# First image loaded and normalised first, VectorE's order fixed until the first attention, relative logits and convolution in turn in pieces twice as long

## The chip, the cores and the metric

The kernel runs on one core of a Trainium2 chip. The metric is the device time in microseconds (us) of one execution, the median of several. The core has five engines that run side by side, each with its own queue of instructions that it takes in order: TensorE (PE; its weight loads are listed apart as PEld), VectorE (DVE), ScalarE (ACT), GpSimd (POOL) and SyncE (SP, which here only issues DMA transfers). TensorE writes its results to PSUM, from where VectorE or ScalarE copies them to SBUF.

## What is computed

The input x holds 8 images of 32 x 32 pixels with 256 channels, in float32. Each image goes through two layers. Layer 0 is a group norm, then a 3 x 3 convolution to 192 channels beside a self-attention over the 1024 pixels, with 8 heads of 8 channels, whose logits have relative terms in both directions. Layer 1 is a self-attention over 1024 tokens with 128 channels, and a mixture of 8 experts of which 2 are used per image.

```python
x = x + conv_attn(group_norm(x))
t = to_tokens(x)
t = t + attn(ln(t))
t = t + moe(ln(t))
```

The parts of `conv_attn` that matter here:

```python
conv_out = conv3x3(x, conv_w) + conv_b
k, q, v = split(x @ qkv_w + qkv_b); q = q * 8 ** -0.5
logits = q @ k.T + rel_w(q, key_rel_w) + rel_h(q, key_rel_h)
attn = softmax(logits) @ v
return concat([conv_out, attn @ attn_w + attn_b])
```

## The kernel before

The kernel has a first phase, with both attentions, image by image, and a second phase with the experts for all images. The first phase is software-pipelined over images by hand: the order of TensorE's instructions is exactly the order in which the program is written (`tc.manual_schedule` at L876 with PE alone), while a scheduler with a cost model orders the other engines' instructions when the kernel is built.

Before the loop over images, the program sets up constants and prepares image 0. In the order of the code:

- `load_image(0)` (L112) loads image 0 into the tile T by a DMA that GpSimd issues (L105).
- ACT issues the loads of `qkvw` and of the convolution weights `taps` (1.7 MB, L125). VectorE (L130 to L133) and ScalarE (L134, L135) turn these nine taps into `convw`: sums and differences for a convolution that makes pairs of neighbouring pixels from shared products.
- SP issues the small loads: `kqb`, `vb`, the biases `l0b`, `aw`, layer 1's `wqkv1`, `wo`, `bo`, and at the end (L181) the two relative tables, 2 KB each.
- VectorE makes small selection matrices from the identity (`gsel`, `gavg`, `esel`, `hsel`), and from the relative tables the weights `bdh` and `bdw` (L194). `reld` (L205, L208) holds differences of rows of `bdh`; VectorE and GpSimd make it together. `KM` (L228, L229, GpSimd) holds for each head group a pattern of ones to which 16 small DMAs add the keys (L358).
- `norm_steps(0)`: TensorE transposes image 0 (`tpx`, L270), VectorE copies it out (L271), takes statistics (L275, L277), TensorE averages over groups (`pm`, `pv`), and VectorE writes the normalised image into `gpad` (L299), which has a border for the convolution. GpSimd adds the biases to T (L279).
- `by_tiles` makes the copy x of `gpad` (GpSimd, L320) that `v` needs, `by_pairs` the sums and differences `gdif` for the convolution (L311).
- `input_steps(0)`: keys and queries (`pk`, L334, into `kq`), values (`pvv`, L367), then the relative logits `prel` (L406): 256 small matmuls of 32 rows and 64 columns in four quarters, (width, height) x (half 0, half 1). After each quarter VectorE and ScalarE copy one half each out (L418, L420). The width part `rw` goes to DRAM (`rwd`) and is transposed by TensorE (`tpw`, L431) into `rwq`. Last, it creates the first `Unit`, whose tile F is gathered by 40 DMAs.

Then for each image b, `conv_layer_attention` runs the attention of layer 0 in four units of 512 queries and two head groups each, with the convolution of the image as filler at its two ends. While it ends, `ahead()` normalises image b+1. `attention_layer` then runs layer 1's attention, and its gaps are filled by `fill(us)`: it takes steps from `input_steps(b + 1)` until their listed times add up to `us`. A step of `prel` is listed with 0.7 us and is followed by `conv.run(3)`, three matmuls of image b+1's convolution. So, once per image b = 0 to 6, relative logits and convolution of image b+1 run in turn. A stretch has 16 such turns: a turn has 16 `prel` matmuls and 3 `pc` matmuls of the program. Every float32 matmul stands as two records in the trace, so that a turn shows 32 and 6. In eight of the turns, two transposes `tpn` of layer 1's normalised tokens (L700) stand between. The PSUM tile `pc` holds twelve convolution matmuls; outside `conv_layer_attention` it comes from a pool with one buffer (`po`), so that VectorE must have added it to T (L461 or L463 and twice L467) before the next one starts.

The calls that set where the turns fall are these:

```python
fill(7.5)          # L689, before the tokens are transposed
fill(0.7)          # L702, after each of the 8 token tiles
fill(5.6)          # L706, before queries and keys of layer 1
fill(0.8)          # L812, in the loop over layer 1's scores
```

Pools that matter: `st` has three PSUM buffers, `lg` (which `prel` uses) two, `F` three in SBUF; `taps`, x, `rw`, F, `qkv` and `pr` all take turns in the latter.

Of the kernel before, what the change touches and what calls it, by code (L numbers as in the profile page):

```python
# [9 lines left out]
FP = mybir.dt.float32  # L10
I32 = mybir.dt.int32
AF = mybir.ActivationFunctionType
ALU = mybir.AluOpType
# [3 lines left out]
P = 128  # L17
# [3 lines left out]
KC = C // P  # L21
NH, DH, DK = 8, 8, 64
HG = 4
NG = NH // HG
CO = C - DK
U = 128
E, F = 8, 512
# [8 lines left out]
def kernel(  # L36
# [26 lines left out]
    nc = tc.nc  # L63
    xt = x.rearrange("b h w c -> b (h w) c")
# [26 lines left out]
    with ExitStack() as ph:  # L91
# [11 lines left out]
        def load_image(b):  # L103
            t = work.tile([P, NT, C], FP, tag="T", name="T", bufs=2)
            nc.gpsimd.dma_start(out=t.rearrange("p (r j) c -> p r j c", j=2), in_=xt[b].rearrange("(r p j) c -> p r j c", p=P, j=2))  # L105
            return t
# [9 lines left out]
        def st_tile(name):  # L116
            return ps_st.tile([P, 512], FP, tag="st", name=name)


        qkvw = wp.tile([P, KC, 3 * DK], FP, tag="qkvw", name="qkvw")  # L120
        nc.scalar.dma_start(out=qkvw, in_=qkv_w.rearrange("(k p) o -> p k o", p=P))


        taps = work.tile([P, 4096], FP, tag="F", name="taps", bufs=3)[:, 0 : 9 * KC * CO]
        nc.scalar.dma_start(  # L125
            out=taps.rearrange("p (n o) -> p n o", o=CO), in_=conv_w.rearrange("a b (k p) o -> p (a b k) o", p=P)
        )
        taps = taps.rearrange("p (a b n) -> p b a n", a=3, b=3)
        convw = wp.tile([P, 4, 3, KC * CO], FP, tag="convw", name="convw")
        nc.vector.tensor_tensor(convw[:, 2], taps[:, 0], taps[:, 2], ALU.add)  # L130
        nc.vector.tensor_tensor(convw[:, 0], convw[:, 2], taps[:, 1], ALU.add)
        nc.vector.tensor_tensor(convw[:, 1], convw[:, 2], taps[:, 1], ALU.subtract)
        nc.vector.tensor_scalar(convw[:, 0:2], convw[:, 0:2], 0.5, None, ALU.mult)  # L133
        nc.scalar.copy(convw[:, 2], taps[:, 0])  # L134
        nc.scalar.mul(convw[:, 3], taps[:, 2], -1.0)  # L135
        convw = convw.rearrange("p v a (k o) -> p v a k o", o=CO)

# [10 lines left out]
        nc.sync.dma_start(out=l0b[:, 0, 0:CO], in_=conv_b.partition_broadcast(P))  # L148
        nc.sync.dma_start(out=l0b[:, 0, CO:C], in_=attn_b.partition_broadcast(P))
        aw = wp.tile([DK, DK], FP, tag="aw", name="aw")  # L150
        nc.sync.dma_start(out=aw, in_=attn_w)
# [5 lines left out]
        bo = wp.tile([P, 1, C], FP, tag="bo", name="bo")  # L157
        nc.sync.dma_start(out=bo[:, 0, :], in_=b_o.partition_broadcast(P))


# [14 lines left out]


        rel = []
        for n, table in (("h", key_rel_h), ("w", key_rel_w)):
            M = table.shape[0]
            raw = wp.tile([M, DH], FP, tag=f"raw{n}", name=f"raw{n}")  # L180
            nc.sync.dma_start(out=raw, in_=table)  # L181
            rep = work.tile([P, 2048], FP, tag="pt", name=f"rep{n}", bufs=4)[0:M, 0:P].rearrange(
                "m (r d) -> m r d", d=DH
            )
            nc.vector.tensor_copy(rep, raw.unsqueeze(1).to_broadcast([M, P // DH, DH]))
            pt = st_tile(f"relt{n}")
            nc.tensor.transpose(pt[:, 0:M], rep.rearrange("m r d -> m (r d)"), ident[0:M, 0:M])
            if n == "h":
                bd = work.tile([P, 2048], FP, tag="pt", name="bdh", bufs=4)[:, 0 : M * HG]
                bd = bd.rearrange("p (m h) -> p m h", h=HG)  # L190
            else:
                bd = wp.tile([P, M, HG], FP, tag="bdw", name="bdw")
            for h in range(HG):
                nc.vector.tensor_scalar(bd[:, :, h], pt[:, 0:M], hsel[:, h : h + 1], None, ALU.mult)  # L194
            rel.append(bd)
        bdh, bdw = rel
        bdw = bdw.rearrange("p m h -> p (m h)")

        def half_w(rows, m, k):
            return bdw[rows, (m + 16 * k) * HG : (m + 16 * k + 16) * HG]  # L200


        NM = 48
        reld = wp.tile([P, NM, 16, HG], FP, tag="reld", name="reld")
        nc.gpsimd.tensor_copy(reld[:, :, 0, :], bdh[:, 0:NM, :])  # L205
        for j in range(1, 16):
            eng = nc.vector if j % 2 else nc.gpsimd
            eng.tensor_tensor(reld[:, :, j, :], bdh[:, j : j + NM, :], bdh[:, 0:NM, :], ALU.subtract)  # L208
        reld = reld.rearrange("p m j h -> p m (j h)")

        def half_h(rows, m, k):
            return reld[rows, m + 16 * k, :]

        KM = []
        oh = wp.tile([P, 16 + DH], FP, tag="oh", name="oh")
        nc.vector.tensor_copy(oh[:, 0:1], esel[:, 0:1])  # L220
        nc.vector.tensor_tensor(oh[:, 1:16], esel[:, 1:16], esel[:, 0:1].to_broadcast([P, 15]), ALU.add)
        nc.vector.tensor_copy(oh[:, 16:24], esel[:, 24:32])
        for i in range(NG):
            km = wp.tile([P, 2, 4, P], FP, tag=f"km{i}", name=f"km{i}")
            for a in range(2):
                kv = km[:, a].rearrange("p g (y x) -> p g y x", y=8)
                for g in range(4):
                    nc.gpsimd.tensor_copy(kv[:, g], oh[:, 0:16].unsqueeze(1).to_broadcast([P, 8, 16]))  # L228
                    nc.gpsimd.tensor_tensor(  # L229
                        kv[:, g], kv[:, g], oh[:, 16:24].unsqueeze(2).to_broadcast([P, 8, 16]), ALU.add  # L230
                    )
            KM.append(km)

# [24 lines left out]
        def f_tile(name):  # L258
            return work.tile([P, 2, 4, 512], FP, tag="F", name=name, bufs=3)


# [64 lines left out]
        def input_steps(b, held):  # L326
# [66 lines left out]
            for which in range(2):  # L393
                for half in range(2):
                    prs = lg_tile("prel")
                    for i in range(16):
                        a = half * 16 + i
                        for g in range(NG):
# [6 lines left out]
                            for k in range(2):  # L405
                                nc.tensor.matmul(  # L406
                                    dst[64 * k : 64 * k + 64], lhsT=table(rows, m, k), rhs=mov, start=True, stop=True
                                )
                        if i % 4 == 3 and i < 15:
                            yield 0.7, True  # L410
                    for g in range(NG):
# [9 lines left out]
                    if which == 0 and half == 1:  # L421
                        for g in range(NG):
                            nc.sync.dma_start(out=rwd[g], in_=rw[g])
                    yield 0.7, True

# [449 lines left out]

        with tc.manual_schedule(engines={mybir.EngineType.PE}):  # L876
            held = {}
            for _ in norm_steps(0):
                pass
            held.update(by_tiles())  # L880
            by_pairs()
            for _ in input_steps(0, held):
                pass
            conv = Conv(0)
            means = []
            for b in range(B):
# [26 lines left out]
                def fill(us):  # L913

                    while us > 0:
                        took, small = next(steps, (None, None))
                        if took is None:
                            break
                        us -= took
                        if small:  # L920
                            conv.run(3)

# [287 lines left out]
```

## Time and profile before

| | |
|---|---|
| median of 3 runs | 2516.28 us (2516.07 to 2519.02) |
| profiled execution, its own time | 2525.62 us |
| its span in the trace | 2523.4 us |
| TensorE busy | 2388.8 us, 95% of the span |
| VectorE busy | 1450.5 us, 57% |
| ScalarE busy | 980.1 us, 39% |
| GpSimd busy | 449.8 us, 18% |
| mean granted TensorE clock | 0.982 |

The profile is of one execution, recorded by the chip. The span runs from the first to the last recorded instruction; the execution's own time is 2.2 us longer, and it lies 9.3 us above the median of the timed runs. Times in the timelines are counted from the span's start. Each line of a timeline merges neighbouring instructions of a kind: start, duration, engine, line of the code, operation, output and input tiles with shapes, count, and in brackets how long the engine was idle before it and what released it. The granted clock is the share of full TensorE clock that the chip let through. Matmuls are pipelined, so a matmul's duration is longer than the distance between two starts.

### The profile page before, as it was taken

The page shows a single profiled execution, that of the slowest core. Times are in us where ns is not written, and L with a number is a line of the kernel's source. Part 1 is how long each engine was busy: PE and PEld are TensorE (multiplying, and loading weights), DVE is VectorE, ACT ScalarE, POOL GpSimd, SP SyncE. Part 2 cuts the span into 40 slices and gives each one's busy share as a digit, 9 for nine tenths or more (in the row PEclk, how much of TensorE's full clock was granted, in tenths as well). Part 3 has the DMA queues.
Part 4 walks back from the last instruction along what each step waited for, and adds up shares of the span by engine and source line. Part 5 has one row for each costly group of instructions (what it writes and reads, how often), then busy time and mean ns, then how long its engine had stood idle before and what let it go on. Part 6 is the DMA issues. An engine that isn't in the chain of part 4 may idle for free. (4 is left out here: it accounts for less than half of the span.)

```text
span 2523.4 us, 42411 instructions
## 1 busy us (share of the span) xinstructions
PE 2388.8 (95%) x17657; PEld 1369.0 (54%) x17657; DVE 1450.5 (57%) x2507; ACT 980.1 (39%) x1625; POOL 449.8 (18%) x464
## 2 busy tenths in 40 slices
PE   3999999999999999999999999999999869999998
PEld 2734753475357535643664366436642546666665
DVE  5675377547744874487358735873684434444444
ACT  1065225532553254336333623363346322332222
POOL 6002120302040204010310121012200132222221
PEclk9899999999999999999999989999999879999999
DMA  2440243024202420341044104410430031221110
GB/s 82 91 65 4 50 90 51 7 51 98 40 22 42 96 38 22 61 84 28 23 80 79 15 22 80 78 15 22 84 65 8 1 122 67 75 76 67 67 59 25
DMA packets 73518, 135.86 MB, mean 54 GB/s; under 512 B 12000, under 2 KB 24168, under 8 KB 71280
## 3 DMA queue, kind: packets, MB, share of 16 engines
q1 hardware_dynamic: 67408, 114.42, 21.7%
q0 software_dynamic: 3328, 16.78, 2.0%
q8 instruction: 139, 2.28, 0.4%
q10 hardware_dynamic: 2592, 1.97, 0.3%
q14 instruction: 51, 0.42, 0.1%
HBM read 53.43 MB, written 25.17 MB: 31 GB/s over the span
## 5 line engine op out<-in xcount | busy, mean ns | idle before, releaser
L560 ACT ACTIVATE PT<-st 128x512 f32<-128x512 f32 (+1 forms) x944 | 541.5, 633 | 581.7 <-PE st L552 579.0
L520 DVE TENSOR_REDUCE my<-lg 128x32 f32<-128x1024 f32 x512 | 617.8, 1223 | 159.9 <-PE st L552 126.8
L552 PE MATMUL st<-F,km 32*128 32x512 f32 x2048 | 549.9, 640 | 14.6 <-DMA F<-mb 8.7
L512 PE MATMUL lg<-km,F 24*128 24x512 f32 x2048 | 526.5, 636 | 1.1 <-issue 0.8
L452 PE MATMUL pc<-convw,gdif 128*128 128x192 f32 x1536 | 308.4, 344 | 10.6 <-DVE T L467 10.6
L569 PE MATMUL po<-PT,vall 128*32 128x256 f32 (+1 forms) x3200 | 314.4, 452 | 2.4 <-ACT PT L560 2.4
L452 PEld LDWEIGHTS pc<-convw,gdif 128*128 128x128 f32 x1536 | 250.5, 193 | 79.0 <-issue 72.7
L512 PEld LDWEIGHTS lg<-km,F 24*128 24x128 f32 x2048 | 151.4, 183 | 175.9 <-issue 101.4
L569 PEld LDWEIGHTS po<-PT,vall 128*32 128x32 f32 x3200 | 67.0, 108 | 313.7 <-issue 280.3
L552 PEld LDWEIGHTS st<-F,km 32*128 32x128 f32 x2048 | 179.6, 183 | 92.4 <-issue 42.4
L1123 PE MATMUL phd<-n2T,w 128*128 128x512 f32 x512 | 223.7, 595 | 0.0
L1140 PE MATMUL py<-w,hT 128*128 128x256 f32 x1024 | 223.6, 379 | 0.0
L1140 PEld LDWEIGHTS py<-w,hT 128*128 128x128 f32 x1024 | 194.6, 190 | 33.2 <-issue 7.7
L279 POOL TENSOR_TENSOR T<-T,l0b 128x2048 f32<-128x2048 f32 x8 | 36.2, 4520 | 813.8 <-PE tpx L270 813.8
L1123 PEld LDWEIGHTS phd<-n2T,w 128*128 128x128 f32 x512 | 97.1, 191 | 114.8 <-issue 107.7
L1147 DVE TENSOR_TENSOR r<-py,n 128x256 f32<-128x256 f32 x64 | 27.1, 424 | 214.7 <-PE py L1140 214.6
L784 PE MATMUL po<-pt,qkv 128*128 128x256 f32 x512 | 116.6, 381 | 11.3 <-DVE pt L776 11.3
L1130 ACT ACTIVATE hT<-phd,b1c 128x512 f32<-128x512 f32 x128 | 86.3, 686 | 96.5 <-PE phd L1123 96.3
L762 DVE TENSOR_REDUCE nm<-lg 128x1 f32<-128x1024 f32 x64 | 78.0, 1219 | 72.5 <-PE lg L753 72.5
L753 PE MATMUL lg<-qkv 128*128 128x512 f32 x256 | 119.1, 593 | 0.0
L784 PEld LDWEIGHTS po<-pt,qkv 128*128 128x128 f32 x512 | 96.6, 190 | 36.2 <-DVE pt L776 13.2
L701 POOL TENSOR_TENSOR T<-T,n 128x256 f32<-128x256 f32 x64 | 47.1, 742 | 293.7 <-DVE n L696 293.7
(231 smaller groups left out, 2467.2 us busy)
## 6 DMA issues: line engine op xcount, KB each, us to landing
F<-rh SPq DMA_DIRECT2D x256, 128.0 KB
F<-kq SPq DMA_DIRECT2D x256, 64.0 KB
F<-rwd SPq DMA_DIRECT2D x256, 64.0 KB
w<-in_L_ffn_W_dram SPq DMA_DIRECT2D x32, 512.0 KB
T<-in_x_dram POOLq DMA_DIRECT2D x8, 1024.0 KB, 5.9
rwd<-rw SPq DMA_DIRECT2D x16, 512.0 KB
Td<-T POOLq DMA_DIRECT2D x8, 1024.0 KB, 8.0
T<-Td SPq DMA_DIRECT2D x8, 1024.0 KB
```

The costliest lines, as they stand in the source:

```text
L452: nc.tensor.matmul(pc[:, v, :], lhsT=gflat[:, 2 * pair + v, kc, at : at + P], rhs=convw[:, 2 * pair + v, dy, kc, :], start=i == 0, stop=i ...
L512: nc.tensor.matmul(lg[:, a, :], lhsT=self.F[r : r + 24, a, 0, i * P : (i + 1) * P], rhs=KM[self.g][r : r + 24, a].rearrange("p e k -> p (e ...
L520: nc.vector.tensor_reduce(my[:, :, hl], lg.rearrange("p a (y x) -> p y a x", y=WW), AX.XY, ALU.max)
L552: nc.tensor.matmul(st[:, i, :] if len(heads) > 1 else st, lhsT=KM[self.g][r : r + 32, a, e, :], rhs=self.F[r : r + 32, a, e, :], start=Tru ...
L560: nc.scalar.activation(self.pts[j][:, hs, :], st, AF.Exp)
L569: nc.tensor.matmul(self.po[32 * hl : 32 * hl + 32, cols], lhsT=vall[:, j, h * (DH + 1) : h * (DH + 1) + 32], rhs=self.pts[j][:, hl, cols], ...
L753: nc.tensor.matmul(lg[:, h, :], lhsT=qk[0][:, i * P : (i + 1) * P], rhs=qk[1][:, h * 512 : (h + 1) * 512], start=True, stop=True,)
L762: nc.vector.tensor_reduce(nm, lg, AX.X, ALU.max, negate=True)
L784: nc.tensor.matmul(po[:, 0:IB], lhsT=v1[:, jc, :], rhs=pt[:, jc, :], start=jc == 0, stop=jc == NT - 1)
L1123: nc.tensor.matmul(phd, lhsT=ws[k][0][:, kc, f * P : (f + 1) * P], rhs=n2T[:, kc, q * 512 : (q + 1) * 512], start=kc == 0, stop=kc == KC - 1,)
L1130: nc.scalar.activation(hT[:, k * NF + f, :], phd, AF.Gelu, bias=b1c[:, f, k * B + b : k * B + b + 1])
L1140: nc.tensor.matmul(py, lhsT=hT[:, k * NF + f, j * P : (j + 1) * P], rhs=ws[k][1][:, f, :], start=k == 0 and f == 0, stop=k == TOPK - 1 and ...
```

## The change

The change has two parts. The first concerns the start. Image 0 is loaded by SP instead of GpSimd, as SP's first DMA. The two relative tables are loaded by ACT as its first DMAs, and `taps` moves behind `qkvw`, after the small loads. The work on tables, key patterns and convolution weights is put into functions (`tables`, `key_patterns`, `conv_weights`) that are called in a new order: the tables `bdh` and `bdw`, the norm of image 0, x, the key patterns, the first four steps of `input_steps(0)`, then `reld`, then `gdif`, then the rest of `input_steps(0)`, and at the end the convolution weights. For all of this VectorE's order too is now the order of the code, as TensorE's is; from the loop over images on, TensorE's alone is.

The second part concerns the turns: a step of `prel` now has eight of the 32 rows or columns instead of four, is listed with 1.4 us, and is followed by `conv.run(6)`.

```diff
         def load_image(b):
             t = work.tile([P, NT, C], FP, tag="T", name="T", bufs=2)
-            nc.gpsimd.dma_start(out=t.rearrange("p (r j) c -> p r j c", j=2), in_=xt[b].rearrange("(r p j) c -> p r j c", p=P, j=2))
+            eng = nc.gpsimd if b else nc.sync
+            eng.dma_start(
+                out=t.rearrange("p (r j) c -> p r j c", j=2), in_=xt[b].rearrange("(r p j) c -> p r j c", p=P, j=2)
+            )
             return t
...
+        raws = []
+        for n, table in (("h", key_rel_h), ("w", key_rel_w)):
+            raw = wp.tile([table.shape[0], DH], FP, tag=f"raw{n}", name=f"raw{n}")
+            nc.scalar.dma_start(out=raw, in_=table)
+            raws.append((n, raw))
         qkvw = wp.tile([P, KC, 3 * DK], FP, tag="qkvw", name="qkvw")
         nc.scalar.dma_start(out=qkvw, in_=qkv_w.rearrange("(k p) o -> p k o", p=P))
...
+        def tables():
...
+            for n, raw in raws:
...
+                nc.vector.tensor_copy(rep, raw.unsqueeze(1).to_broadcast([M, P // DH, DH]))
+                pt = st_tile(f"relt{n}")
+                nc.tensor.transpose(pt[:, 0:M], rep.rearrange("m r d -> m (r d)"), ident[0:M, 0:M])
...
+                for h in range(HG):
+                    nc.vector.tensor_scalar(bd[:, :, h], pt[:, 0:M], hsel[:, h : h + 1], None, ALU.mult)
...
+            def reld_steps():
+                nc.gpsimd.tensor_copy(reld4[:, :, 0, :], bdh[:, 0:NM, :])
+                for j in range(1, 16):
+                    eng = nc.vector if j % 2 else nc.gpsimd
+                    eng.tensor_tensor(reld4[:, :, j, :], bdh[:, j : j + NM, :], bdh[:, 0:NM, :], ALU.subtract)
...
+        def key_patterns():
...
+        def conv_weights(taps):
+
+            taps = taps.rearrange("p (a b n) -> p b a n", a=3, b=3)
+            convw = wp.tile([P, 4, 3, KC * CO], FP, tag="convw", name="convw")
+            nc.vector.tensor_tensor(convw[:, 2], taps[:, 0], taps[:, 2], ALU.add)
+            nc.vector.tensor_tensor(convw[:, 0], convw[:, 2], taps[:, 1], ALU.add)
+            nc.vector.tensor_tensor(convw[:, 1], convw[:, 2], taps[:, 1], ALU.subtract)
+            nc.vector.tensor_scalar(convw[:, 0:2], convw[:, 0:2], 0.5, None, ALU.mult)
+            nc.scalar.copy(convw[:, 2], taps[:, 0])
+            nc.scalar.mul(convw[:, 3], taps[:, 2], -1.0)
...
-                        if i % 4 == 3 and i < 15:
-                            yield 0.7, True
+                        if i == 7:
+                            yield 1.4, True
...
-                    yield 0.7, True
+                    yield 1.4, True
...
-        with tc.manual_schedule(engines={mybir.EngineType.PE}):
+        with tc.manual_schedule(engines={mybir.EngineType.PE, mybir.EngineType.DVE}):
             held = {}
+            half_w, half_h, reld_steps = tables()
             for _ in norm_steps(0):
                 pass
             held.update(by_tiles())
+            KM = key_patterns()
+            steps = input_steps(0, held)
+            for _ in range(4):
+                next(steps)
+            reld_steps()
             by_pairs()
-            for _ in input_steps(0, held):
+            for _ in steps:
                 pass
+            convw = conv_weights(taps)
+        with tc.manual_schedule(engines={mybir.EngineType.PE}):
             conv = Conv(0)
...
                         if small:
-                            conv.run(3)
+                            conv.run(6)
```

## What is expected of it, before it ran

> **What bounds the kernel now.** I read the page's busy shares first: TensorE holds 95% of the span, VectorE 57%. Time is therefore saved only where TensorE stands still, or works on something that need not be there. The page's 40 slices show one slice in which it stands still: the first 63 us have PE digit 3.
>
> ```profile
> PE   3999999999999999999999999999999869999998
> ```
>
> Next, the timeline of the first 90 us (start us, us busy, engine, line, instruction, count, idle before and releaser).
>
> ```profile
> 1.50 0.95 POOL L105 DMA_DIRECT2D T<-in_x_dram  x1
> ...
> 19.16 0.22 DVE L185 COPY reph<-rawh 63x128 f32<-63x128 f32 x1 [19.16 <-DMA rawh<-in_L_conv_key_rel_h_dram]
> ...
> 31.50 2.34 DVE L271 COPY xT<-tpx 128x1024 f32<-128x1024 f32 x2
> ...
> 40.47 6.49 DVE L299 TENSOR_SCALAR gpad<-xT,gm,gr 128x1024 f32<-128x1024 f32 x2
> 41.13 4.49 POOL L279 TENSOR_TENSOR T<-T,l0b 128x2048 f32<-128x2048 f32 x1
> ...
> 73.70 2.90 PE L452 MATMUL pc<-convw,gdif 128*128 128x192 f32 x12
> ...
> 81.19 4.87 PE L452 MATMUL pc<-convw,gdif 128*128 128x192 f32 x18
> ```
>
> VectorE starts at 19.16, when a 2 KB table lands that was queued behind 0.8 MB of weights. It then works on convolution weights and tables (L130 to L222), and reaches the image (tpx had it in PSUM at 28.2) only at 31.5. The normalised image, gpad, is whole at 46.96; the first convolution piece starts at 73.5, the second, after waits for F, at 81.19.
>
> The second place is the stretch in which the next image's relative logits (prel) alternate with convolution (pc), once per image b=0 to 6. TensorE's timeline of the first, then its weight loads (PEld):
>
> ```profile
> 270.71 1.24 PE L452 MATMUL pc<-convw,gdif 128*128 128x192 f32 x6
> 271.88 0.67 PE L406 MATMUL prel<-kq,reld 32*64 32x32 f32 x32
> 273.34 1.21 PE L452 MATMUL pc<-convw,gdif 128*128 128x192 f32 x6 [0.80 <-DVE T L467]
> ```
>
> ```profile
> 265.40 0.95 PEld L452 LDWEIGHTS pc<-convw,gdif 128*128 128x128 f32 x6
> 266.57 0.56 PEld L406 LDWEIGHTS prel<-kq,reld 32*64 32x64 f32 x32 [0.23 <-issue]
> 267.17 0.95 PEld L452 LDWEIGHTS pc<-convw,gdif 128*128 128x128 f32 x6
> ```
>
> A turn (six pc records, 32 prel records) lasts 1.77 us, of which 0.23 goes at pc to prel and 0.04 at prel to pc. Twice per stretch pc waits for VectorE to empty its PSUM tile. Finally the clock, from the stretches table (the last columns are granted clock, DMA share, GB/s):
>
> ```profile
> 56.00:58.00 2.00, 2.00 (x128) 2.00 (x132) 0.69 (x1) 0.00 (x0) 0.96 (x1) 1.00 0.16 33
> 58.00:60.00 2.00, 1.14 (x56) 1.04 (x49) 1.05 (x1) 0.64 (x1) 0.00 (x0) 0.56 0.13 25
> 247.70:279.70 32.00, 30.48 (x625) 26.34 (x625) 10.30 (x20) 4.79 (x8) 10.42 (x9) 1.00 0.13 43
> ```
>
> Image 0's prel, with no convolution between, runs at full clock for some 2.4 us (128 records in 2.00 us, 15.6 ns each), then at half until about 75; the alternating stretch keeps full clock.
>
> [...] gpad, 0.81 us alone, took 6.49 for two beside GpSimd's 4.49 us add. [...]
>
> **The start, step by step.** The sum is made in the profiled execution (span 2523.4, its own time 2525.62), which is 9.3 us above the median of 2516.28; I carry the saving over unchanged.
>
> (a) Loads. T is now SP's first issue, near 0.7, on a hardware queue; taps (1.7 MB) becomes ACT's fourth. Between 6 and 14 us the engines moved about 350 GB/s, so T's 1 MB takes 3 us alone; it shares with taps from about 4 us. Estimate: T lands at 8. Before, it landed 12.1 us after issue, at 13.6. VectorE's order is fixed, and its second instruction, kqbs, waits for kqb, which SP queues behind T: everything on VectorE waits until about 8.3. Bounds: 6.5 (T undisturbed) and 16 (when all loads had landed before).
>
> (b) The twelve lines from gsel to bdw cost 3.1 us by the timeline, with one trip to TensorE 0.6. The transpose reltw stands ahead of tpx in TensorE's order, so tpx runs from 10.9: 16 at 0.24 = 3.9 us, first half done at 12.9.
>
> (c) Norm: twice (copy 1.2, two stats 1.3, aggregate 0.2) = 5.4, to 18.2; from the last aggregate to gpad 3.9 as before (36.54 to 40.47), to 22.1. The T add now starts when tpx ends, 14.8, and is over at 19.3, so it no longer sits on gpad; reld on GpSimd (0.53 + 7 x 0.65) does, until 24.4. Two gpad: 1.6 alone, 6.5 at worst, I take 2.3: gpad is whole at 24.4, which is 22.6 us earlier.
>
> (d) From gpad to the convolution before: 26.5 us. Now GpSimd begins x only when reld and the load of image 1 (0.9) are issued, 25.3; with 6.46 of copies pvv ends near 32.3, about as far after gpad as before. On VectorE reld (8 x 0.58) and gdif (2.9) stand between the first and second kq, then vall: free at 38. The first two prel quarters are ready by 36 to 38, so their copies run 38 to 41, and the third quarter, which needs a PSUM tile back, starts at 40 to 41. Third and fourth took 7.9 before (half clock): 48. tpw 3.7: 51.6. The convolution weights, hidden earlier under loads and tables, now come last on VectorE: 4 x 1.34 = 5.4 after the last rwq copy, to 57.4. TensorE idles 6 us there, and pc starts at 57.4 instead of 73.5: 16.1 us earlier.
>
> (e) F. GpSimd's key patterns (9.6 before) now follow x: done by 42 to 43; SP's km transfers wait for them and end near 46, rwd 47, the 16 first F issues at 0.7 end at 58.5, landed at 60.5. The lg waits seen before at 78.4 and 80.2 (0.8 and 0.3 on TensorE, after a longer gap at 76.5) mostly go. Second pc piece at about 62.7 instead of 81.19. **Start: 18.5 us saved**, bounds 11 (kqb lands at 16) and 24 (kqb at 6.5, no stall for vall).
>
> **The turns.** Before, 32.0 us from first prel to tpw: 8 turns with tpn at 2.04, 8 without at 1.77, two pc waits of 0.76. After: eight turns, each with one tpn. prel 64: 0.62 + 0.56 = 1.18; pc 12: 0.92 + 0.95 = 1.87; tpn and gap 0.47; together 3.52, times 8 = 28.2. That prel stays at 17.5 ns in a run of 64 follows from the 128 at 15.6 ns. The pc waits shrink: VectorE needs 1.35 after a piece (L463, two L467), plus one n (0.41) now between, and TensorE brings tpn and 64 prel (1.65) first; I leave 0.15 each, 0.3.
>
> Each fill(0.7) now takes 1.4, so the prel pieces are used up by the eighth tile and all four tpw groups go ahead of pq, where two went before. They cost 2.4 (the st tiles wait for ACT) against 0.9. pq thus starts 30.9 after the first prel against 32.9: 2.0 saved. Before, the other two tpw groups ran at 294.45 under ACT's exponential (ends 295.57), so their removal there gains nothing directly; TensorE idles 1.5 instead. But their copies delayed nm by 0.6 there: 0.4 more. F of the next unit is issued earlier, into a slot x or an old F has left; SP is idle then. Per image 2.4, bounds 1.0 (the idle and the st waits eat it) and 3.4; seven images: **16.8 us saved**, 7 to 24.
>
> The attention loops, the feed-forward part and image 7 have the same order as before: nothing.
>
> **Sum:** 18.5 + 16.8 = 35.3; profiled execution 2490.3, median 2516.28 - 35.3 = **2481 us**.
>
> **Rivals.** (1) The start gives half: VectorE's fixed order stalls, because kqb lands late behind T and taps, or vall and kq hold back the prel copies longer. For: strict order, second place. Against: kqb is small. 9 us from the start, 2490. (2) The longer turns give nothing: tpw uncovered and more st waits eat the saved switches. For: TensorE idles more after the scores. Against: the 0.23 at each switch is plain. 2498. (3) Slower: the clock. [...] it halves the clock in each of seven stretches as it did at 58.3, for 17 us (58.3 to 75). Price: 8.5 us each, 60; 2481 + 60 = 2541. It decides if bursts of 1.2 us suffice; image 0 needed 2.4 with no large matmul between, while here 1.9 us of pc follow.
>
> **Numbers.** Forecast (25 to 46 saved, 2470 to 2491) 0.58; rival 1 0.17; rival 2 0.15; rival 3 0.06; more than 46 saved, both bounds met, 0.04. The range 2466 to 2499 leaves out rival 3 and the worse half of 2. All but rival 3 lie clearly under 2511, the line of 0.2% (5 us, about what a measurement of this kernel can tell): faster 0.93, same 0.01, slower 0.06.
>
> **What would show it.** Right: T lands near 8, gpad is whole near 24, TensorE idles some 6 us before a first pc near 57, the second pc is near 63; prel stretches of some 30 us to pq, at full clock, with 64 prel per turn, no 0.8 us waits for L467. Wrong: VectorE's first wait lasting to 16, gpad again beside a GpSimd add, clock under 1.00 in the stretches, or a stretch as long as before.

## The result, and the profile after

The changed kernel takes 2482.26 us (median of 4 runs, 2479.95 to 2484.59), the kernel before 2516.18 us beside it (4 runs, 2515.87 to 2519.02). The ratio is 0.9863, with a 95% interval from 0.9846 to 0.988: 33.9 us saved. The forecast was 2481.

The page of the changed kernel's profiled execution (2482.71 us, span 2480.2). First the row of busy tenths of TensorE, then TensorE's convolution matmuls: busy time, mean ns, idle time before them and what ended most of it.

```profile
PE   5999999999999999999999999999998869999998
...
L472 PE MATMUL pc<-convw,gdif 128*128 128x192 f32 x1536 | 289.0, 337 | 9.7 <-DVE convw L276 6.2
```

The first digit was 3 and is 5, the others are nearly as before. The idle time before the convolution now has one large cause, the wait for its weights at the start.

The timeline of the start (start us, us, engine, line, instruction, count, idle before and its releaser):

```profile
0.73 0.43 SPq L106 DMA_DIRECT2D T<-in_x_dram  x1
2.54 6.08 DVE L213 COPY reph<-rawh 63x128 f32<-63x128 f32 x1 [2.54 <-DMA rawh<-in_L_conv_key_rel_h_dram]
4.81 3.74 POOL L195 MEMSET gdif<- 128x4352 f32 x1
10.46 3.68 PE L290 MATMUL tpx<-ident,T 128*128 128x128 f32 x16
14.23 4.51 POOL L299 TENSOR_TENSOR T<-T,l0b 128x2048 f32<-128x2048 f32 x1 [5.69 <-PE tpx L290]
21.52 1.81 DVE L319 TENSOR_SCALAR gpad<-xT,gm,gr 128x1024 f32<-128x1024 f32 x2
58.25 4.18 PE L472 MATMUL pc<-convw,gdif 128*128 128x192 f32 x12 [6.20 <-DVE convw L276]
64.92 3.19 PE L472 MATMUL pc<-convw,gdif 128*128 128x192 f32 x18
```

The normalised image is whole at 23.33 (46.96 before). The two writes of gpad take 1.81 us in place of 6.49; GpSimd's add on T (4.51 us) is over at 18.74, before they start. The second convolution piece starts at 64.92 (81.19 before). The 6.08 us of reph, a copy whose twin repw takes 0.21, is new.

A turn of the stretch in which relative logits and convolution alternate, on TensorE and in its weight loads:

```profile
489.20 0.38 PE L720 MATMUL tpn<-ident,n 128*128 128x128 f32 x2
489.51 1.13 PE L426 MATMUL prel<-kq,reld 32*64 32x32 f32 x64
490.57 2.22 PE L472 MATMUL pc<-convw,gdif 128*128 128x192 f32 x12
492.63 0.38 PE L720 MATMUL tpn<-ident,n 128*128 128x128 f32 x2
...
497.81 2.19 PE L472 MATMUL pc<-convw,gdif 128*128 128x192 f32 x12 [0.31 <-DVE T L487]
```

```profile
489.51 1.02 PEld L426 LDWEIGHTS prel<-kq,reld 32*64 32x64 f32 x64 [0.17 <-ACT rw L440]
490.57 1.92 PEld L472 LDWEIGHTS pc<-convw,gdif 128*128 128x128 f32 x12
```

A turn lasts 3.43 us (489.20 to 492.63), against 2.04 and 1.77, 3.81, for the two it replaces. Its weight loads wait once, 0.17 us, at the change to prel, and pc's waits for VectorE are 0.20 and 0.31 us per stretch in place of 0.72 to 0.80. The clock (us of the stretch, TensorE's busy time and records, granted clock, DMA share, GB/s):

```profile
35.00:40.00 5.00, 3.19 (x121) 0.54 0.04 8
41.40:48.30 6.90, 6.90 (x256) 0.50 0.18 45
60.00:65.00 5.00, 4.78 (x17) 0.73 0.58 82
65.00:70.00 5.00, 5.00 (x31) 1.00 0.57 68
```

Image 0's relative logits start at 32.61, at a clock of 1.00; from about 35 to about 63 us the clock is still about half (0.57 over the whole of it), except for some 3 us in TensorE's idle time before the convolution (1.00 from 52.6 to 55.8). From 41.40 to 48.30 TensorE works on these small matmuls without a gap, at 0.50.

Marks on TensorE's timeline make a measure that is finer than the whole time. In us, from the starts of the instructions (stretch: first prel to first tpw; tail: first tpw to first pq; period: one image's first output projection pp to the next one's, the usual value of the run):

| | first pp | stretch | tail | period |
|---|---|---|---|---|
| before | 238.62 | 31.99 | 0.87 | 244.65 |
| changed | 220.68 | 28.39 | 2.20 | 242.08 |

So in these two traces the start brings 17.9 us and each of seven images 2.57, 18.0 together. From the last pp to the end nothing changes (564.8 and 564.5). These 35.9 us are more than the medians' 33.9, and two things blur such a sum. Single half-clock events, of 1.7 us where they fall on the keys and queries pk (5.24 us in place of 3.55 from their first start to that of the values pvv, at a mean clock of 0.67), are spread over the executions: the changed kernel's first period, 245.32, holds two of 1.5 to 1.7 us. The profiled execution before had two on pk and one stretch of 37.24 us in place of 31.99, at a mean clock of 0.85 in place of 1.00 (a period of 252.61), together 9.7 us, which would account for the 9.3 by which it lay above its median.

The first pp, too, is less fixed than the table looks. Six traces have the start of the changed kernel (the one above, run 10, which repeats it, and runs 1, 3, 4 and 5). In them the first convolution starts at 58.12 to 58.33, but the clock from 62 to 100 us is anything from 0.99, here, to 0.88, in run 3:

```profile
62.00:100.00 38.00, 37.78 (x227) 0.99 0.56 77
62.00:100.00 38.00, 38.00 (x206) 0.88 0.56 77
```

Their first pp comes at 220.57 to 224.19. Against the one trace of the kernel before, the start is thus worth 14 to 18 us, and a difference of up to 3.6 us in one trace's first pp says little.

### The profile page after: what moved, and what is told of

It reads as the page before. It is cut to its first block, busy times and chain, and to the rows that moved or that the text cites. A ratio compares the mean times of both kernels' runs of the same rounds, so it can differ in the third digit from the quotient of the medians.

```text
span 2480.2 us, 42408 instructions
## 1 busy us (share of the span) xinstructions
PE 2362.5 (95%) x17657; PEld 1359.1 (55%) x17657; DVE 1452.0 (59%) x2507; ACT 981.8 (40%) x1625; POOL 449.4 (18%) x463
## 5 line engine op out<-in xcount | busy, mean ns | idle before, releaser
L472 PE MATMUL pc<-convw,gdif 128*128 128x192 f32 x1536 | 289.0, 337 | 9.7 <-DVE convw L276 6.2
```

The lines of the kernel that those rows point to most:

```text
L472: nc.tensor.matmul(pc[:, v, :], lhsT=gflat[:, 2 * pair + v, kc, at : at + P], rhs=convw[:, 2 * pair + v, dy, kc, :], start=i == 0, stop=i ...
```

## The experiments

Twelve runs, one of them of the changed kernel again, each with four to six executions. The executions of the kernel before beside them spread from 2514.0 to 2540.1 us; beside runs 6 to 9 their median was 2533.1, beside the others 2516.4 to 2522.5, and why is not known. From run 3 on the variants are therefore compared with the changed kernel. Their own executions spread by 1.7 to 10 us, so differences of 2 to 4 us are read from periods and from single waits in the traces, not from the medians alone.

**1 and 2. Each part alone.** The start alone, in the changed kernel:

```diff
-                        if i == 7:
-                            yield 1.4, True
+                        if i % 4 == 3 and i < 15:
+                            yield 0.7, True
...
-                            conv.run(6)
+                            conv.run(3)
```

> The changed kernel with its pieces set back to 32 relative-logit matmuls and 3 convolution steps, so only the part at the start is left. If the two parts add, as the sum of the prediction has them, this saves the start's share alone: 17 to 18.5 us, 2498 to 2499 us against 2516, and the stretches from the first relative-logit matmul to the transposes of rw are 32.0 us again in every image. The rival, that the trace's 17.9 us at the first output projection came partly from the longer pieces or from clock events in the profiled run, gives less: 2504 us or more.

2501.72 us (2498.68 to 2508.87), ratio 0.9943 [0.993, 0.9957]: 14.7 us. The stretch is 32.03 again, the first pp at 222.18, 16.4 us early. In its profile (2508.87) the convolution matmuls of image 2's stretch took nearly twice their time, as at half clock:

```profile
749.85 1.08 PE L426 MATMUL prel<-kq,reld 32*64 32x32 f32 x32
750.86 2.29 PE L472 MATMUL pc<-convw,gdif 128*128 128x192 f32 x6
```

Six pc took 1.21 us in the kernel before. The turns alone, in the kernel before, are the same edit the other way:

> The kernel before with the longer pieces alone (64 relative-logit matmuls, then 6 convolution steps). If the turns are worth what the trace of the changed kernel shows, 2.3 to 2.6 us in each of seven images, this saves 16 to 18 us: 2498 to 2500 us, with the stretch at 28.4 us and 2.2 us of transposes uncovered after it. The rival, that a part of the gain hangs on the new start or that the longer run of small matmuls lowers the granted clock, gives a saving under 12 us (2504 or more) and half-clock pieces in the stretch.

2499.25 us (2498.31 to 2499.97), ratio 0.993 [0.9917, 0.9944]: 17.2 us. Stretch 28.37, tail 2.20, period 242.1, as expected; the first pp comes 1.9 us later than before (240.56), as the clock from 75 to 100 us is 0.86 in place of 0.93, which makes 1.8. The two savings sum to 31.9 us, the change's is 33.9 with 4 us of interval to each side: they add, within what can be measured. The start's expectation was missed by 2.7 us, and its rival (2504 or more) did not hold either; the fastest run, 2498.68, lies where the sum has it.

**3. Pieces twice as long again**: one prel piece per quarter, of 64 matmuls of the program, 128 records in the trace, then 12 convolution steps.

```diff
-                        if i == 7:
-                            yield 1.4, True
...
-                    yield 1.4, True
+                    yield 2.8, True
...
-                            conv.run(6)
+                            conv.run(12)
```

> The changed kernel with pieces twice as long again: 128 relative-logit matmuls, then 12 convolution steps, so four pieces in an image and four rounds of switching less. If a switch between the two kinds of work costs what the first doubling shows (8 switch pairs and their waits saved 3.6 us in the stretch, 0.45 us each), four fewer save up to 1.8 us in the stretch and up to 1.8 x 7 = 12 us in the whole, to about 2470; if most of those 3.6 us were the waits on VectorE's copies, of which only 0.2 to 0.3 us per stretch is left, about 0.25 x 4 x 7 = 7 us, to 2475. The rival, that 128 of these matmuls in a row (some 4.4 us at half a microsecond per 16) bring the granted clock down to half inside the piece, makes it equal or slower: 2482 to 2500.

2485.5 us (2485.05 to 2487.76): no gain, 3 us over the changed kernel. The stretch did shrink, 28.39 to 25.59, and at full clock (1.00 from 470 to 500 us); the clock rival, whose range the time fits, is wrong. But of these 2.80 us, where at most 1.8 were expected, a part is only moved: the stretch no longer holds the transposes of four of the eight token tiles. The tail grew from 2.20 to 5.53, and the period is 242.55 in place of 242.08. The timeline shows what was not expected:

```profile
502.06 1.39 PE L449 MATMUL tpw<-ident,rw 128*128 128x128 f32 x8
503.28 0.32 PE L718 MATMUL tpn<-ident,n 128*128 128x128 f32 x1
503.76 0.33 PE L718 MATMUL tpn<-ident,n 128*128 128x128 f32 x1 [0.16 <-ACT rwq L453]
...
505.56 0.66 PE L449 MATMUL tpw<-ident,rw 128*128 128x128 f32 x4 [0.68 <-ACT rwq L453]
...
507.32 0.44 PE L718 MATMUL tpn<-ident,n 128*128 128x128 f32 x2 [0.67 <-DVE n L714]
```

Four pieces are used up after the fourth of eight token tiles. The other tiles' transposes (tpn) then have only tpw groups between them and wait for VectorE and ScalarE. The pieces are the cover of the second normalisation; eight of them are as few as eight tiles can do with.

**4. The uncovered transposes of rw** put back behind the scores: the third fill goes.

```diff
-            fill(5.6)
             whole()
```

> The changed kernel without the third call that fills TensorE in the second layer's preparation, so that two of the four groups of rw transposes fall into the first gap between scores and transposes of the second layer, as in the kernel before. If those groups cost their own time where they lie now, uncovered before the second layer's projections (2.2 us there against 0.9), and the gap of about 1.1 us before the first score transposes is idle otherwise, this saves 0.9 to 1.2 us per image, 6 to 8 us in all: 2474 to 2476. The rival, that the gap is needed anyway because the softmax on ScalarE, slowed by the copies of those transposes, ends it, gives no change within 2 us.

2476.58 us (2475.79 to 2483.2), ratio 0.9844 [0.9831, 0.9858]. Tail 1.22, period 241.5 where the clock is full. Before the first score transposes, the changed kernel and then this one:

```profile
516.19 3.60 PE L773 MATMUL lg<-qkv 128*128 128x512 f32 x8
520.87 1.09 PE L793 MATMUL tp<-ident,pr 128*128 128x128 f32 x8 [1.08 <-ACT pr L784]
```

```profile
519.11 1.04 PE L451 MATMUL tpw<-ident,rw 128*128 128x128 f32 x8
520.38 1.13 PE L792 MATMUL tp<-ident,pr 128*128 128x128 f32 x8 [0.23 <-ACT pr L783]
```

The idle 1.08 is used, 0.23 is left. That is 0.6 us per image, 4 us in all, where 6 to 8 were expected: from the first score transposes to the next pp the image is 0.3 us longer (187.53 against 187.23), which was not traced further.

**5. The same with one group in each of the first two gaps**: the fill in the loop over scores is 0.4 in place of 0.8 as well.

> The changed kernel without the third fill, as in the run with the transposes of rw put later, and with one of the two late groups in each of the first two gaps between scores and transposes of the second layer instead of both in the first. If TensorE waits for the softmax in both gaps, 0.4 to 1.1 us of wait each take one group whole: the stretch from the first score transposes to the next output projection loses the 0.3 us per image that the two groups in one gap cost (187.5 against 187.2), and the time is 2 us under that run's 2476.6: 2473 to 2476. If the second gap holds no wait, its group costs its own 0.4 us and the time is 2476 to 2480. The first image's stretch is untouched by it.

2482.94 us (2479.43 to 2483.7), period 241.65: outside both expectations; no better than the run before, and by its median no better than the changed kernel. The first gap still waits, 0.67 us with one group in it, and the second group finds no wait (its tp come without one) and costs its own time. The periods of 4 and 5 are both 0.4 to 0.6 us under the changed kernel's; the whole times, 6.4 us apart at nearly equal periods, show how little a median of five runs tells here.

**6. GpSimd's clearing of gdif cut** to the border rows:

```diff
-        nc.gpsimd.memset(gdif, 0.0)
+        nc.gpsimd.memset(gdif[:, :, :, 0 : HH + 2 : HH + 1, :], 0.0)
```

> The changed kernel with gdif's clearing on GpSimd cut to the two border rows that nothing else writes (256 elements per partition instead of 4352, so about 0.2 us instead of 3.74). Theory: VectorE's first copy (reph, 6.08 us long in the changed kernel's trace, 0.21 for its twin repw) was held until GpSimd's clearing ended. Then reph ends within 0.4 us of the end of the last large clearing, near 5.2 us instead of 8.6, and the transposes of the image start at 7.0 to 9 us instead of 10.46, by what the landing of kqb and T still holds; the whole is 1.5 to 3.5 us faster than the changed kernel. Rival, the wait that the prediction named: kqb behind the image on SP's queue holds VectorE; then reph ends and the transposes start where they do now and the time does not change.

The timeline of its start:

```profile
2.20 3.00 DVE L213 COPY reph<-rawh 63x128 f32<-63x128 f32 x1 [2.20 <-DMA rawh<-in_L_conv_key_rel_h_dram]
4.81 0.33 POOL L195 MEMSET gdif<- 128x256 f32 x1
7.31 0.16 DVE L137 TENSOR_TENSOR kqbs<-kqb,kqs 128x1 f32<-128x1 f32 x1 [2.10 <-DMA kqb<-in_L_conv_qkv_b_dram]
9.61 3.67 PE L290 MATMUL tpx<-ident,T 128*128 128x128 f32 x16
```

reph ends at 5.20, when the last clearing ends (5.14): the clearing had held it. But kqb is the second lock, to 7.31, so the image's transposes start only 0.85 us earlier, at 9.61 and not at 7.0 to 9. The whole takes 2481.28 us (2480.21 to 2482.12), as the changed kernel does (2482.26, and 2481.20 in run 10). The first convolution starts at 55.55 in place of 58.25 (VectorE's work on reld and gdif took 5.7 us in place of 9.9), yet the first pp at 222.15 in place of 220.68. Its clock:

```profile
62.00:100.00 38.00, 38.00 (x215) 0.92 0.54 75
```

In the changed kernel the same stretch has 0.99. The missing 0.07 of 38 us is 2.7 us, as much as the lead. In one trace that could be chance, since the same start had 0.88 to 0.99. But over the whole execution, five of this kernel's six have a mean clock of 0.981 or 0.982, and the nine of the changed kernel 0.982 to 0.985; so most of them seem to lose it, and why was not isolated.

**7. The convolution weights earlier**, after the copies of rw:

```diff
-            for _ in steps:
-                pass
-            convw = conv_weights(taps)
+            for n, _ in enumerate(steps):
+                if n == 11:
+                    convw = conv_weights(taps)
```

> The changed kernel with the convolution weights computed after the copies of rw in VectorE's order, where VectorE sits idle for 3.96 us, instead of after the last copies of rwq. Theory: TensorE's 6.20 us of idle time before the first convolution is wholly the wait for these four operations; then that idle goes, the first convolution starts at 52 to 53 us instead of 58.25, the two copies of rh move by at most 1.5 us, and the kernel is 4 to 6 us faster than the changed one. Rival: the wait hides behind others (the first scores, which need the F tile by DMA, start at 62.4 us anyway), and the idle time only moves behind the convolution: under 1.5 us.

2484.8 us (2482.9 to 2486.28): the rival is right. From its timeline:

```profile
40.99 5.63 DVE L273 TENSOR_TENSOR convw<-taps 128x1152 f32<-128x1152 f32 x1
41.27 4.12 POOL L331 TENSOR_TENSOR gdif<-gpad 128x512 f32<-128x512 f32 x4
...
52.43 2.22 PE L472 MATMUL pc<-convw,gdif 128*128 128x192 f32 x12 [0.31 <-ACT rwq L455]
55.80 1.09 PE L532 MATMUL lg<-km,F 24*128 24x512 f32 x2 [1.15 <-DMA F<-kq]
63.49 3.70 PE L532 MATMUL lg<-km,F 24*128 24x512 f32 x6 [6.61 <-DMA F<-rwd]
```

The convolution starts 5.8 us earlier, and the idle time moves behind it, before the scores: SP issues the 16 loads of F at 0.65 us each from 51.3 on, behind the copies of rh, of which VectorE's end at 51.87 in place of 49.21. One operation on the weights took 5.63 us in place of 1.35 beside GpSimd's gdif. The clock from 62 to 100 is 0.86 in this trace. The other five executions have a mean clock of 0.983 to 0.985, as the changed kernel has, and still take 2482.9 to 2486.28, so the clock alone does not explain the time.

**8 and 9. Which part of the start's change does it**: VectorE's order left to the scheduler, and the first image on GpSimd's queue.

```diff
-        with tc.manual_schedule(engines={mybir.EngineType.PE, mybir.EngineType.DVE}):
+        with tc.manual_schedule(engines={mybir.EngineType.PE}):
```

> The changed kernel with only TensorE's order written out at the start, VectorE's left to the scheduler. Its order then puts two of the eight operations on reld ahead of the image's first copy, six into the normalisation, and three of the four on the convolution weights before gpad is whole: 8 x 0.70 + 3 x 1.35 = 9.6 us of VectorE time between the landing of the image and gpad. Theory: the order is the larger part of the start's gain, and gpad is whole 6 to 9 us later than 23.3 us; the convolution weights are then ready early, which gives back up to 6 us at the first convolution, so the first output projection is 1 to 5 us later and the whole 2483 to 2488. Rival: GpSimd's order sets gpad anyway and the new order of VectorE gives under 1 us.

2494.69 us (2493.97 to 2495.08), 12.4 us over the changed kernel; first pp 235.01. The order is the larger part of the start's gain, but not as expected (2483 to 2488): gpad is whole at 27.2, 3.9 us late and not 6 to 9. Most of the loss comes from GpSimd, whose order nobody wrote:

```profile
18.70 0.78 POOL L262 COPY km<-oh 128x128 f32<-128x128 f32 x2
...
36.59 3.87 POOL L238 TENSOR_TENSOR reld<-bdh 128x192 f32<-128x192 f32 x7
40.39 0.97 POOL L106 DMA_DIRECT2D T<-in_x_dram  x1
41.37 4.29 POOL L340 COPY x<-gpad 128x128 f32<-128x128 f32 x16
41.84 0.69 PE L387 MATMUL pvv<-qkvw,x 128*128 128x64 f32 x2 [10.00 <-POOL x L340]
```

VectorE makes oh early there, at 8.93 in place of 23.25, so the scheduler lets GpSimd build the key patterns, then reld, ahead of x; TensorE waits 10.00 us for x, and the first convolution starts at 67.61, 9.4 us late. An order fixed on VectorE had fixed GpSimd's through oh.

```diff
-            eng = nc.gpsimd if b else nc.sync
+            eng = nc.gpsimd
```

> The changed kernel with the first image loaded by GpSimd's queue again, all else as changed. Its issue lies first in GpSimd's program by the code, or behind its clearing of tiles if the scheduler puts it there. Theory: the queue matters little, since 1 MB lands about 5 us after its issue on either; the transposes of the image start within 1 us of 10.46 us and the time stays within 2 us of the changed kernel, so that the start's gain comes from the order on VectorE and from the weights that no longer go ahead. Rival: GpSimd's queue holds the image as before; then transposes start 5 us later or more and the time is 2487 or more.

2486.24 us (2483.97 to 2487.22), 4 us over the changed kernel, between the two expectations. T lands at 11.72, 10.2 us after its issue and not about 5; on SP's queue it was there by 7.06 (run 12). VectorE's tables hide most of this, so the transposes start at 11.76, after a wait for T of 5.16 us, 1.3 us later than in the changed kernel. Further on, pvv waits 2.32 us for GpSimd's copies of x, but the first convolution starts only 1.2 us later, at 59.40. The second piece starts 4.7 us later, at 69.58, with a wait of 1.37 us for F and a clock of 0.90 from 62 to 100; these were not separated. The loads on ACT's queue, the third part of the start's change, were not undone by themselves. Two lines show once more what holds VectorE's copies:

```profile
4.09 2.03 POOL L191 MEMSET gpad<- 128x2312 f32 x1
4.45 1.74 DVE L213 COPY repw<-raww 63x128 f32<-63x128 f32 x1
7.42 0.15 DVE L137 TENSOR_TENSOR kqbs<-kqb,kqs 128x1 f32<-128x1 f32 x1
```

repw takes 1.74 us, 0.21 in the changed kernel, and ends at 6.19, when gpad's clearing ends (6.12). kqbs, which only has small inputs and isn't a copy, runs in 0.15 us beside gdif's clearing (6.05 to 9.86).

**10 to 12. What the runs point to.** One more measure of the changed kernel, then the weights in two halves (two operations before VectorE's first kq, two after rh) with F loaded head by head, then these with the edits of 4 and 6 and kqb ahead of the image.

> The changed kernel itself, as the measure for the two others on the same chip. If its time depends on the chip as little as 2482.3 and the runs of one part suggest, 2480 to 2485 us; if the kernel before is again at 2530 here, this tells how far the changed kernel suffers from what slows it.

2481.20 us (2479.95 to 2483.26); first pp 220.57, period 242.05.

```diff
-                for a in range(2):
-                    for hl in range(HG):
+                for hl in range(HG):
+                    for a in range(2):
                         r = 32 * ((hl + 2 * a) % HG)
...
+            weights = conv_weights(taps)
+            next(weights)
+            next(weights)
             steps = input_steps(0, held)
...
+                if n == 15:
+                    convw = next(weights)
```

> The changed kernel with two edits at the start of the first attention: two operations on the convolution weights before VectorE's first copy of kq (where it waits 3.19 us) and two after the last copies of rh; and in every F tile the loads issued head by head (both key halves of a head together) instead of key half by key half. Theory: after the weights, what held TensorE in the run with early weights was SP's queue, 16 loads of F at 0.65 us each, of which the first scores need the first and the ninth or tenth; head by head the first scores need 4 to 8 of them, so they start at 54 to 57 us instead of 62.4 and the idle 6 us before the first convolution goes for good: 4 to 6 us faster than the changed kernel. Rival: the halved clock at the start and the loads that follow take it back, as with the early weights alone: within 1.5 us of the changed kernel or slower.

2481.93 us (2481.21 to 2486.36): no gain; first pp 226.10. The six idle us before the first convolution are gone, but the two operations placed in VectorE's idle time cost GpSimd nearly as much:

```profile
23.82 1.35 DVE L274 TENSOR_TENSOR convw<-taps 128x1152 f32<-128x1152 f32 x1
24.71 10.52 POOL L342 COPY x<-gpad 128x128 f32<-128x128 f32 x16
33.47 6.66 PE L389 MATMUL pvv<-qkvw,x 128*128 128x64 f32 x30 [4.61 <-POOL x L342]
```

The 16 copies of x take 10.52 us in place of 4.44, now beside a VectorE at work nearly without a gap from 23.82 to 33.6; TensorE waits 4.61 us, and prel starts at 40.06 in place of 32.61. The first convolution is then 0.7 us ahead (57.53), the first scores start at 60.06, not at 54 to 57, and wait twice more for F, and the second piece is 1.0 us late (65.93). The rest of the 5.4 us by which the first pp is late goes with the clock: 0.91 in place of 0.99 from 62 to 100 makes 3.0 us, and 0.92 in place of 1.00 over the last 21 us before it some 1.7.

> All that the runs point to in one kernel: the edits of the run before, the short clearing of gdif, kqb loaded ahead of the image, and no third fill. If they add, 5.7 us for the transposes of rw, 4 to 6 for weights and F, and 2 to 3.5 for the first copies on VectorE (the transposes of the image at 7 to 7.5 us instead of 10.46) make 2467 to 2471; if the start's gains are lost behind one another, only the 5.7 us remain: 2475 to 2477.

2479.47 us (2475.75 to 2482.45), ratio 0.9835 [0.9811, 0.9859], outside both expectations. The transposes start at 7.06 without a wait, as expected (10.46 before), but gpad is whole at 22.6, only 0.7 us early:

```profile
18.07 1.16 ACT L280 ACTIVATE convw<-taps 128x1152 f32<-128x1152 f32 x1 [14.15 <-DMA taps<-in_L_conv_conv_w_dram]
20.55 0.20 ACT L317 ACTIVATE gr<-gr 128x2 f32<-128x2 f32 x1
```

ScalarE has a copy for the convolution weights ahead of the root that the norm needs, and taps lands 3.3 us later than in the changed kernel; image 1's load, issued by GpSimd at 10.83 in place of 23.72, runs beside it, which is the likely cause and was not tried by itself. First pp 222.73, period 241.4. The first convolution starts at 54.78 (58.25), the second piece at 63.99 (64.92), and the clock from 62 to 100 is 0.91: of the three gains only that of run 4 is left in this trace. No version has an earlier first pp than the changed kernel. Run 4 has the lowest median; its gain of some 4 us rests on the periods.

## Why the prediction was right

**The sum.** 35.3 us were forecast, 18.5 and 16.8. The trace has 17.9 and 18.0; the medians, 33.9. The two parts alone gave 14.7 and 17.2. The start was put somewhat too high and the turns somewhat too low, so that their errors offset in part; that the sum came within 1.4 us of the medians is in part luck.

**(a) Loads.** T was to land at 8; it had landed by 7.06 (run 12). VectorE was to be held to 8.3 by kqb, behind the image on SP. It was held to 8.62, but by reph, which GpSimd's clearing, over at 8.55, blocked; kqb, at 7.3, came second (run 6). The number was right by luck, and its cause wrong. The 6.49 us of gpad beside GpSimd's add was taken into account for the new gpad, and not for reph beside GpSimd's clearings.

**(b), (c) Transposes and norm.** tpx forecast 10.9, came at 10.46; last aggregate 18.2 and 17.91; gpad 24.4 and 23.33, with 1.81 us for the two writes (2.3 taken).

**(d) To the convolution.** Third prel quarter forecast 40 to 41, came at 41.40; idle of 6 us before a first convolution at 57.4, came as 6.20 before 58.25. The ends differ by less than 1.5 us, but terms inside are off both ways: on VectorE reld and gdif took 5.59 and 4.32 us in place of 4.6 and 2.9, on GpSimd the copies of x 4.44 in place of 6.46.

**(e) F.** Second convolution piece forecast 62.7, came at 64.92: 16.3 us earlier than before in place of 18.5. The 16 issues of F's loads ended at 60.60, forecast 58.5, and the scores before that piece waited for F. At the first pp the saving is 17.9, because the kernel before had half clock past 80 us in its trace (0.93 from 75 to 100, 1.8 us); this brought the start near its forecast by chance.

**The turns.** Stretch forecast 28.5, 28.39 measured; the tail 0.9 to 2.4, measured 0.87 to 2.20; the gain from the removed groups behind the scores 0.4, measured 0.3 (187.52 to 187.23). The pc waits were put at 0.3 in all and are 0.51. Per image 2.57 in place of 2.4, the better by 1.2 us over seven.

**The rivals.** Half a start (2490) and no gain from the turns (2498) are refuted by the marks; runs 1 and 2 show either part alone at 14 us or more. The clock rival (2541) is refuted: no stretch with pieces of 64 or 128 ran at half clock, in 84 stretches of twelve traces (1.00 in all seven of the changed kernel), while 2 of the 14 with pieces of 32 did, at least in part (before, 0.85 over the stretch, and start alone, by its matmuls of 2.29 us in place of 1.21). That the longer pieces prevent it is not shown by so few; it agrees with the narrow runs of the turns alone (1.7 us from lowest to highest) beside the 3.8 us of the kernel before.

**What the sum left out.** The half clock at the start was carried over as equal in both kernels. But it differs from execution to execution, by up to 3.6 us at the first pp for one and the same start, so a trace of each kernel does not fix the start's gain to better than that. In the traces of runs 6 and 7 it makes 2.7 and 4.9 us.

## What to carry to other kernels

Work out a start engine by engine, with the order of each queue, and look at what GpSimd does in the same microseconds as VectorE: an operation put into idle time of VectorE can go with a loss on GpSimd, and through it on TensorE, nearly as large as what it saves (run 11: copies of x of 10.52 us in place of 4.44, and 4.61 us of waiting for them on TensorE). Pieces of filler work are best as long as the places they cover are many: doubling eight and eight was worth 3.6 us a stretch, and doubling once more uncovered the work between. When single clock events of 2 to 8 us come and go, compare periods of a loop and single waits before medians, and take a mark that occurs once per execution from several traces.

## What was not expected of the hardware

- GpSimd's clearing of a tile, which reads nothing, held a VectorE copy from SBUF to SBUF, of 0.22 us in the kernel before, for 6.08 us, over two clearings in a row (2.04 and 3.74 us), and one for 1.74 us in run 9, until a single clearing ended. VectorE's scaling of relth out of PSUM beside clearings (run 9) took 0.90 us, as in the changed kernel, where GpSimd stands idle at that time (9.14 to 10.04).
- TensorE at 100% busy with 32-row matmuls stayed at half clock (41.40 to 48.30 us: 6.90 of 6.90 busy, 0.50). In the same trace the clock was whole from 65 us on (1.00 from 65 to 100, TensorE busy for all of these 35 us), with convolution and score matmuls since 58.25. The same busy share thus stood beside half and beside full clock; what raises the clock was not shown.
- The clock after the start differs between executions of the same start: from 62 to 100 us it was 0.88 to 0.99 in six traces with a first convolution at 58.12 to 58.33. Kernels that reach the convolution earlier, at 55.55, 54.78 and 52.43, had 0.92, 0.91 and 0.86, but one that reaches it later, at 59.40, had 0.90. That an earlier start costs clock is not shown, and what sets the time at which the clock comes back was not isolated.
